# First stage of a decoder layer: all its loads on one queue in order of use, and keys, then values of three context tiles ahead of the norm of x

## The chip, the core and the metric

The kernel runs on one core of a Trainium2 chip. The core has five engines with a queue of instructions each: TensorE (PE in the profile, with its weight loads as PEld), VectorE (DVE), ScalarE (ACT), GpSimd (POOL) and SyncE (SP), which here only issues transfers. Each engine takes its own queue strictly in order; between engines there are semaphores. Transfers (DMAs) are issued from the queues of SP, ACT and POOL and are carried by 16 DMA engines that the core's queues share. Matmul results go to PSUM banks, which DVE or ACT must empty before PE can write them again.

The metric is the device time of one execution, in microseconds (us), as the median of several runs. Clock figures in the profile are shares of TensorE's full speed as granted to it.

## What is computed

One decoder layer on x of 16 x 64 x 512 numbers (n, c, l) and a context of 16 x 64 x 512, all float32. Cut to what matters:

```
xn = layernorm(x)                                   # over l
q  = transpose(xn, (2, 0, 1))                       # l, n, c
p  = softmax(einsum('lnc,lmc->lnm', q, q) / 8)      # 512 small attentions of 16 rows
x  = x + xn + transpose(einsum('lnm,lmc->lnc', p, q), (1, 2, 0))

h  = layernorm(x)
k  = rmsnorm(ctx @ Wk.T) * k_norm_w                 # 1024 rows, 8 heads of 128
v  = ctx @ Wv.T
qq = rmsnorm(h @ Wq.T) * q_norm_w                   # 32 heads of 128
x  = x + softmax(qq k / sqrt(128)) v @ Wo.T         # four query heads for each key head

x  = x + mixture_of_experts(layernorm(x))           # 16 experts, 4 for a row, and a shared one
```

The change concerns the first five lines and the lines of k and v: everything that runs before the queries of the second attention.

## The kernel before

All names are of one function, `decoder_layer`. The 1024 rows of context are cut into 8 tiles of 128 rows (NT = 8), each held with the contracted 512 on the partitions in four chunks (DC = 4). A scheduler places the instructions: program order sets dependencies and priorities, and the scheduler moves what is ready ahead in each engine's queue, so that for instance a matmul of a later tile can stand between the steps of an attention. The queues it fixes are then executed in order.

**Loads.** x goes to `xs`: partitions 0 to 63 take c with the first half of l, partitions 64 to 127 c with the second half. Eight transfers of 256 KB do it (line 133), issued from ACT's queue (S). On SP's queue (nc.sync) go context tile 0 (line 124), the key weights `wk_sb` in two halves of 1 MB (line 130), context tile 1, the value weights `wv_sb` in two halves (line 140), then the query weights of groups 0 and 1 (line 168). Each half of wk or wv holds 512 columns, that is four of the eight heads. POOL's queue loads small constants. Context tiles lie in a pool of two buffers (`two`, tag "ctx"), so tile i + 2 can be loaded when tile i has been used.

**`keys_values(i)`** works on context tile i: eight matmuls (two halves of four) against wk (line 213), whose two results ACT squares (line 218) and DVE sums and copies (lines 219, 220); eight matmuls against wv (line 224), whose results ACT copies (line 228); then the keys' root mean square (lines 230 to 232), eight transposes (line 236) and ACT's scaled copies into `kT` (line 237). A float32 matmul appears in the profile as two recorded passes, so 8 matmuls are `x16` there; a float32 transpose is one record. The results take turns in three PSUM banks (`mm_bank`).

**`split_norm`** is the layer norm of x. DVE takes statistics of each of 16 n (lines 176, 177); since a row's 512 numbers lie half on one partition and half on another, a small matmul joins the two halves' means (line 181), and a second one their deviations (line 189); ACT takes the root (line 191), DVE the reciprocal (line 193) and the 16 normalizations (line 199). The first call writes `xg`, the layout in which all 16 n of eight neighbouring l stand together, so that an attention can start only after the last of the 16. After each, POOL adds the normalized part to xs (line 298).

**`batch_attention(q)`** runs 64 of the 512 small attentions: transposes of xf (line 251), scores (line 259), scaling and maximum on DVE (lines 264, 269), exponentials on ACT (line 272), division on DVE (lines 276, 277), transposes of the probabilities (line 283), ACT's copy (line 285), products (line 287) and DVE's addition to xs (line 292). There are eight calls.

**The order of the stage**: keys_values(0), the norm of x, keys_values(1), then four times an attention, keys_values(i + 2) and another attention; POOL then sends xs away (lines 308, 309), `split_norm` runs again into xn, the query weights are loaded, keys_values(6) and (7) follow, and xn is transposed to `xnT` (line 319), from which the queries are computed (line 357). The expert stage at the end has lines from 760 on.

Of the kernel before, what the change touches and what calls it, by code (L numbers as in the profile page):

```python
# [23 lines left out]
F32 = mybir.dt.float32  # L24
# [5 lines left out]
P = 128  # L30
N, C, L = 16, 64, 512
NT = N * C // P
DC = L // P
# [15 lines left out]
def decoder_layer(  # L49
# [24 lines left out]
    nc = tc.nc  # L74
    V, S, T, G = nc.vector, nc.scalar, nc.tensor, nc.gpsimd
# [4 lines left out]
    wqp = ctx.enter_context(tc.tile_pool(name="wqp", bufs=2))  # L80
# [6 lines left out]
    def bank(tag, bufs):  # L87
        return psum.tile([P, 512], F32, tag=tag, name=tag, bufs=bufs)

    def mm_bank():  # L90
        return bank("mm", 3)

    def tr_bank():
        return bank("tr", 2)

    def sc_bank():
        return bank("sc", 3)
# [6 lines left out]
    v = [p.tile([P, NT, KVH // 2 * HD], F32, tag="v", name="v") for p in (kvp0, kvp)]  # L104
# [6 lines left out]
    two = p1.enter_context(tc.tile_pool(name="two", bufs=2))  # L111
# [5 lines left out]
    wk_sb = one.tile([P, DC, KVH * HD], F32, tag="wk", name="wk_sb")  # L117
    wv_sb = one.tile([P, DC, KVH * HD], F32, tag="wv", name="wv_sb")

    ctx_tiles = {}  # L120

    def load_ctx(i):
        ct = two.tile([P, DC, P], F32, tag="ctx", name="ct")
        nc.sync.dma_start(ct, ctxt[i])
        ctx_tiles[i] = ct

    load_ctx(0)
    for h in range(2):
        cols = slice(h * 512, (h + 1) * 512)
        nc.sync.dma_start(wk_sb[:, :, cols], wk[:, :, cols])  # L130
    for q in range(4):
        for h in range(2):
            S.dma_start(
                xs[h * C : (h + 1) * C, 4 * q : 4 * q + 4, :],
                x[4 * q : 4 * q + 4, :, h * LH : (h + 1) * LH].rearrange("n c l -> c n l"),
            )
    load_ctx(1)
    for h in range(2):
        cols = slice(h * 512, (h + 1) * 512)
        nc.sync.dma_start(wv_sb[:, :, cols], wv[:, :, cols])  # L140

    ident = const.tile([P, P], F32, tag="ident", name="ident")
    make_identity(nc, ident)
# [22 lines left out]
    def load_wq(g):  # L166
        w = wqp.tile([P, DC, GRP * HD], F32, tag="wq", name="wq_sb")
        nc.sync.dma_start(w, wq[g])
        wq_tiles[g] = w
# [31 lines left out]
            )  # L201


    def keys_values(i):
        ct = ctx_tiles.pop(i)
        if i + 2 < NT:
            load_ctx(i + 2)
        kraw = two.tile([P, KVH, HD], F32, tag="kraw", name="kraw")
        ss = small.tile([P, KVH], F32, tag="ss", name="ss")
        for h in range(2):  # L210
            kp = mm_bank()
            for d in range(DC):
                T.matmul(  # L213
                    kp, ct[:, d, :], wk_sb[:, d, h * 512 : (h + 1) * 512],
                    start=(d == 0), stop=(d == DC - 1),
                )
            kh = kraw[:, 4 * h : 4 * h + 4, :]
            S.activation(kh.rearrange("p h d -> p (h d)"), kp, AF.Square)
            V.tensor_reduce(ss[:, 4 * h : 4 * h + 4], kh, AX.X, ALU.add)
            V.tensor_copy(kh.rearrange("p h d -> p (h d)"), kp)  # L220
        for h in range(2):
            vp = mm_bank()
            for d in range(DC):
                T.matmul(  # L224
                    vp, ct[:, d, :], wv_sb[:, d, h * 512 : (h + 1) * 512],
                    start=(d == 0), stop=(d == DC - 1),
                )
            S.copy(v[h][:, i, :], vp)
        rk = small.tile([P, KVH], F32, tag="rk", name="rk")
        S.activation(rk, ss, AF.Sqrt, bias=eps_sb, scale=1.0 / HD)  # L230
        V.reciprocal(rk, rk)
        V.tensor_mul(kraw, kraw, rk.unsqueeze(2).to_broadcast([P, KVH, HD]))
        for h in range(2):
            tp = tr_bank()
            for j in range(4):
                T.transpose(tp[:, j * P : (j + 1) * P], kraw[:, 4 * h + j, :], ident)
            S.activation(
                kT[h][:, :, i * P : (i + 1) * P],
                tp.rearrange("p (j t) -> p j t", j=4), AF.Copy, scale=kw_sb,
            )  # L240


    def batch_attention(q):
        g0 = q * GE * LE

        def group(g, rows=slice(0, P)):
            return xf[rows, (q * GE + g) * P : (q * GE + g + 1) * P]

        qp = tr_bank()
        for g in range(GE):  # L250
            T.transpose(qp[:, g * P : (g + 1) * P], group(g), ident)
        qt = two.tile([P, GE, P], F32, tag="qt1", name="qt1")
        S.copy(qt.rearrange("p g c -> p (g c)"), qp)
        probs = []
        for h in range(2):
            hs = slice(h * C, (h + 1) * C)
            sp = sc_bank()
            for g in range(GE):
                T.matmul(
                    sp[:, g * P : (g + 1) * P], group(g, hs), group(g, hs),  # L260
                    start=True, stop=True,
                )
            pr = two.tile([P, GE, P], F32, tag="pr", name="pr", bufs=3)
            V.scalar_tensor_tensor(
                pr, sp.rearrange("p (g m) -> p g m", g=GE), C**-0.5,
                blocks_sb.unsqueeze(1).to_broadcast([P, GE, P]), ALU.mult, ALU.add,
            )
            nm = small.tile([P, GE], F32, tag="nm", name="nm")
            V.tensor_reduce(nm, pr, AX.X, ALU.max, negate=True)
            rs = small.tile([P, GE], F32, tag="rs", name="rs")  # L270
            for g in range(GE):
                S.activation(
                    pr[:, g, :], pr[:, g, :], AF.Exp, bias=nm[:, g : g + 1],
                    accum_out=rs[:, g : g + 1],
                )
            V.reciprocal(rs, rs)
            V.tensor_mul(pr, pr, rs.unsqueeze(2).to_broadcast([P, GE, P]))
            probs.append(pr)
        mp = sc_bank()
        for h in range(2):  # L280
            tp = tr_bank()
            for g in range(GE):
                T.transpose(tp[:, g * P : (g + 1) * P], probs[h][:, g, :], ident)
            pt = two.tile([P, GE, P], F32, tag="pt1", name="pt1")
            S.copy(pt.rearrange("p g n -> p (g n)"), tp)
            for g in range(GE):
                T.matmul(
                    mp[h * C : (h + 1) * C, g * P : (g + 1) * P],
                    qt[:, g, h * C : (h + 1) * C], pt[:, g, :], start=True, stop=True,
                )  # L290
        xv = xs[:, :, g0 : g0 + GE * LE].rearrange("p n (g e) -> p g n e", e=LE)
        V.tensor_add(xv, mp.rearrange("p (g n e) -> p g n e", g=GE, e=LE), xv)

    keys_values(0)
    split_norm(lambda n: xg[:, :, n, :], xs)
    for n in range(N):
        xv = xs[:, n, :].rearrange("p (g e) -> p g e", e=LE)
        G.tensor_add(xv, xv, xg[:, :, n, :])
    keys_values(1)
    for i in range(4):  # L300
        batch_attention(2 * i)
        keys_values(i + 2)
        batch_attention(2 * i + 1)
    for h2 in range(2):
        for h in range(2):
            rows, cols = slice(h2 * C, (h2 + 1) * C), slice(h * LH, (h + 1) * LH)
# [3 lines left out]
    split_norm(lambda n: xn[:, n, :], xs)  # L310
    load_wq(0)
    load_wq(1)
    keys_values(6)
    keys_values(7)
    for n0 in range(0, N, 4):
        for k in range(2):
            tp = tr_bank()
# [696 lines left out]
```

## Time and profile before

| what | value |
|---|---|
| median of 3 runs | 1096.88 us (1095.32 to 1097.59) |
| the profiled execution: its time | 1095.54 us |
| its span (first to last instruction) | 1093.8 us |
| mean granted clock of TensorE | 0.966 |
| PE busy, 0 to 20 us | 6.13 us |
| PE busy, 20 to 40 us | 15.34 us |
| PE busy, 40 to 60 us | 14.37 us |
| PE busy, 160 to 200 us | 39.34 of 40 us |
| first transposes of xn (line 319) | 194.16 us |
| first statistics of x on DVE (line 176) | 12.09 us |
| ACT's issues of x (line 133) | 0.75 to 15.5 us |

The span runs from the first to the last recorded instruction, and the time lies 1.74 us above it. Times within the profile are counted from the span's start. A row of a timeline gives the start, the duration, engine, line and operation, `out<-in` with the sizes, how many instructions were merged into it, and in brackets how long the engine had stood idle before it and what released it. A row of a windows table gives for a stretch of time its length, then busy time and number of instructions of PE, PEld, DVE, ACT and POOL, and then the granted clock, the busy share of the DMA engines and what they moved in GB/s. Matmuls are pipelined, so a busy engine need not run at its peak.

### The profile page before, as it was taken

The page shows a single profiled execution, that of the slowest core. Times are in us where ns is not written, and L with a number is a line of the kernel's source. Part 1 is how long each engine was busy: PE and PEld are TensorE (multiplying, and loading weights), DVE is VectorE, ACT ScalarE, POOL GpSimd, SP SyncE. Part 2 cuts the span into 40 slices and gives each one's busy share as a digit, 9 for nine tenths or more (in the row PEclk, how much of TensorE's full clock was granted, in tenths as well). Part 3 has the DMA queues.
Part 4 walks back from the last instruction along what each step waited for, and adds up shares of the span by engine and source line. Part 5 has one row for each costly group of instructions (what it writes and reads, how often), then busy time and mean ns, then how long its engine had stood idle before and what let it go on. Part 6 is the DMA issues. An engine that isn't in the chain of part 4 may idle for free. (4 is left out here: it accounts for less than half of the span.)

```text
span 1093.8 us, 13537 instructions
## 1 busy us (share of the span) xinstructions
PE 1007.2 (92%) x4556; PEld 704.4 (64%) x4556; DVE 533.7 (49%) x1112; ACT 414.7 (38%) x1130; POOL 344.5 (31%) x356
## 2 busy tenths in 40 slices
PE   3799999799999999999999989879799999999974
PEld 1355554587888888888888867767564455545431
DVE  1735557746664756556564566657567211111100
ACT  1156663255544544445454453332220122222220
POOL 2400001312332424225143342352352443444232
PEclk9999999899999999999999999988789999999997
DMA  9200003110110201102011110000022966655643
GB/s 249 99 20 10 10 10 78 78 40 1 39 40 1 78 1 39 39 34 102 1 39 39 40 39 1 30 30 20 29 33 88 396 155 148 148 122 104 155 106 54
DMA packets 28378, 74.96 MB, mean 69 GB/s; under 512 B 4560, under 2 KB 8704, under 8 KB 26256
## 3 DMA queue, kind: packets, MB, share of 16 engines
q1 hardware_dynamic: 15792, 49.81, 13.4%
q0 software_dynamic: 10336, 22.13, 9.9%
q10 hardware_dynamic: 2176, 2.10, 0.8%
q8 instruction: 38, 0.62, 0.2%
q14 instruction: 36, 0.29, 0.1%
HBM read 98.90 MB, written 16.02 MB: 105 GB/s over the span
## 5 line engine op out<-in xcount | busy, mean ns | idle before, releaser
L886 PE MATMUL sc<-w,xt 128*128 128x512 f32 x288 | 131.6, 601 | 1.4 <-ACT xt L880 1.4
L404 ACT ACTIVATE square<-qraw 128x128 f32<-128x128 f32 x256 | 79.2, 309 | 82.6 <-DVE qraw L398 43.3
L334 POOL TENSOR_TENSOR sat<-at 128x256 f32<-128x256 f32 x32 | 26.2, 818 | 254.6 <-ACT at L474 254.6
L911 POOL DMA_INDIRECT out_dram<-y,idx x36 | 56.8, 1577 | 121.3 <-DMA out_dram<-y,idx 59.3
L886 PEld LDWEIGHTS sc<-w,xt 128*128 128x128 f32 x288 | 52.8, 193 | 55.2 <-issue 53.3
L357 PE MATMUL mm<-wo_t,sat 128*128 128x256 f32 x256 | 70.6, 401 | 13.0 <-POOL sat L335 13.0
L891 DVE TENSOR_TENSOR z<-sc,z 128x256 f32<-128x256 f32 x36 | 15.2, 423 | 132.1 <-ACT z L890 132.1
L357 PE MATMUL mm<-wq_t,xns 128*128 128x256 f32 x256 | 72.7, 393 | 6.1 <-DVE xns L335 4.7
L357 PE MATMUL mm<-wo_sb,at 128*128 128x256 f32 x256 | 72.8, 406 | 4.3 <-ACT at L474 4.3
L213 PE MATMUL mm<-wk_sb,ct 128*128 128x512 f32 x128 | 62.4, 623 | 14.2 <-DMA wk_sb<-in_wk_dram 14.2
L436 PEld LDWEIGHTS sc<-kT,qt 128*128 128x128 f32 x512 | 62.1, 193 | 19.1 <-ACT qt L421 12.3
L357 PE MATMUL mm<-wq_sb,xnT 128*128 128x256 f32 x256 | 70.5, 381 | 2.6 <-DVE su L396 2.6
L441 DVE SCALAR_TENSOR_TENSOR prob<-sc,mask_sb 128x512 f32<-128x512 f32 x32 | 22.0, 687 | 103.8 <-PE sc L436 103.8
L436 PE MATMUL sc<-kT,qt 128*128 128x64 f32 x512 | 69.4, 282 | 1.6 <-ACT qt L421 1.4
L906 PE MATMUL mm<-w,zt 128*128 128x512 f32 x144 | 68.2, 596 | 2.6 <-DVE zt L899 2.1
L224 PE MATMUL mm<-wv_sb,ct 128*128 128x512 f32 x128 | 60.5, 612 | 9.9 <-DVE kraw L220 6.9
L357 PEld LDWEIGHTS mm<-wo_t,sat 128*128 128x128 f32 x256 | 50.6, 200 | 22.3 <-POOL sat L335 15.2
L357 PEld LDWEIGHTS mm<-wo_sb,at 128*128 128x128 f32 x256 | 51.2, 205 | 13.2 <-ACT at L474 6.3
L357 PEld LDWEIGHTS mm<-wq_t,xns 128*128 128x128 f32 x256 | 47.5, 194 | 12.2 <-POOL wq_sb L344 4.9
L890 ACT ACTIVATE z<-sc 128x256 f32<-128x256 f32 x36 | 13.8, 383 | 108.4 <-PE sc L886 108.4
L906 PEld LDWEIGHTS mm<-w,zt 128*128 128x128 f32 x144 | 26.9, 190 | 35.8 <-issue 32.1
L870 POOL DMA_INDIRECT xg<-rows_d,idx x38 | 37.2, 980 | 39.9 <-DVE weight L840 18.2
(252 smaller groups left out, 2030.8 us busy)
## 6 DMA issues: line engine op xcount, KB each, us to landing
w<-in_wg_dram SPq DMA_DIRECT2D x38, 512.0 KB
w<-in_wu_dram SPq DMA_DIRECT2D x38, 512.0 KB
w<-in_wd_dram SPq DMA_DIRECT2D x38, 512.0 KB
wq_sb<-in_wq_dram SPq DMA_DIRECT2D x8, 1024.0 KB
wo_sb<-in_wo_dram SPq DMA_DIRECT2D x8, 1024.0 KB
ct<-in_ctxt_dram SPq DMA_DIRECT2D x8, 256.0 KB
xs<-in_x_dram ACTq DMA_DIRECT2D x8, 256.0 KB
wk_sb<-in_wk_dram SPq DMA_DIRECT2D x2, 1024.0 KB
```

The costliest lines, as they stand in the source:

```text
L213: T.matmul(kp, ct[:, d, :], wk_sb[:, d, h * 512 : (h + 1) * 512], start=(d == 0), stop=(d == DC - 1),)
L224: T.matmul(vp, ct[:, d, :], wv_sb[:, d, h * 512 : (h + 1) * 512], start=(d == 0), stop=(d == DC - 1),)
L334: engine.tensor_add(s[:, 0], a21, a22)
L357: T.matmul(dst, left[:, k, :], right[:, k, :], start=k == 0, stop=k == 1)
L404: S.activation(square, raw[:, h, :], AF.Square, accum_out=q_ss[g][:, 2 * u + j, h : h + 1])
L436: T.matmul(sp[:, at : at + C], qt[:, b, 2 * hp : 2 * hp + 2, :], kT[g // 4][:, g % 4, k0 : k0 + C], start=True, stop=True,)
L441: V.scalar_tensor_tensor(pr, sp.rearrange("p (a k) -> p a k", a=8), HD**-0.5, mask_sb.unsqueeze(1).to_broadcast([P, 8, C]), ALU.mult, ALU.add,
L870: G.indirect_dma_start(xg, None, rows_d, bass.IndirectOffsetOnAxis(idx[:, b : b + 1], axis=0))
L886: T.matmul(hp, xt[:, d, :], w1_tiles[buffer(j)][:, :, d, :], start=(d == 0), stop=(d == DC - 1))
L891: V.tensor_mul(z, hp[:, FI:], z)
L906: T.matmul(op, zt[:, c, :], w2_tiles[buffer(j)][:, c, :], start=(c == 0), stop=(c == FI // P - 1))
L911: G.indirect_dma_start(out, bass.IndirectOffsetOnAxis(idx[:, b : b + 1], axis=0), y, None, bounds_check=NT * P - 1, oob_is_err=False, comp ...
```

## The change

All loads of the first stage are issued on SP's queue, in the order in which they are used: context 0, the first half of wk in four pieces of 256 KB (one for each chunk of the contracted dimension), its second half, context 1, half of x, context 2, the rest of x, wv, contexts 3 to 5. Four context tiles get a place of their own, `ctx_early`, which is one of the two buffers of the pool of query weights (8 KB on each partition); the second load of query weights into that buffer must wait until they have been used.

`keys_values` is parted into `keys(i)` and `values(i)`. Keys of tiles 0, 1, 2, then values of 0, 1, 2 now stand ahead of the norm of x. Tiles 3, 4 and 5 follow after the second, fourth and sixth attention in program order, tiles 6 and 7 after the second norm, keys first.

```diff
+    ctx_early = wqp.tile([P, 4, DC, P], F32, tag="wq", name="ctx_early")
+
     def load_ctx(i):
-        ct = two.tile([P, DC, P], F32, tag="ctx", name="ct")
+        ct = ctx_early[:, i] if i < 4 else two.tile([P, DC, P], F32, tag="ctx", name="ct")
         nc.sync.dma_start(ct, ctxt[i])
         ctx_tiles[i] = ct
 
+    halves_of = [slice(h * 512, (h + 1) * 512) for h in range(2)]
     load_ctx(0)
-    for h in range(2):
-        cols = slice(h * 512, (h + 1) * 512)
-        nc.sync.dma_start(wk_sb[:, :, cols], wk[:, :, cols])
+    for d in range(DC):
+        nc.sync.dma_start(wk_sb[:, d, halves_of[0]], wk[:, d, halves_of[0]])
+    nc.sync.dma_start(wk_sb[:, :, halves_of[1]], wk[:, :, halves_of[1]])
+    load_ctx(1)
     for q in range(4):
         for h in range(2):
-            S.dma_start(
+            nc.sync.dma_start(
                 xs[h * C : (h + 1) * C, 4 * q : 4 * q + 4, :],
                 x[4 * q : 4 * q + 4, :, h * LH : (h + 1) * LH].rearrange("n c l -> c n l"),
             )
-    load_ctx(1)
-    for h in range(2):
-        cols = slice(h * 512, (h + 1) * 512)
+        if q == 1:
+            load_ctx(2)
+    for cols in halves_of:
         nc.sync.dma_start(wv_sb[:, :, cols], wv[:, :, cols])
+    for i in range(3, 6):
+        load_ctx(i)
...
-    def keys_values(i):
-        ct = ctx_tiles.pop(i)
-        if i + 2 < NT:
-            load_ctx(i + 2)
+    def keys(i):
+        ct = ctx_tiles[i]
         kraw = two.tile([P, KVH, HD], F32, tag="kraw", name="kraw")
...
+    def values(i):
+        ct = ctx_tiles.pop(i)
+        if 4 <= i < NT - 2:
+            load_ctx(i + 2)
+        for h in range(2):
+            vp = mm_bank()
+            for d in range(DC):
+                T.matmul(
+                    vp, ct[:, d, :], wv_sb[:, d, h * 512 : (h + 1) * 512],
+                    start=(d == 0), stop=(d == DC - 1),
+                )
+            S.copy(v[h][:, i, :], vp)
...
-    keys_values(0)
+    for part in (keys, values):
+        for i in range(3):
+            part(i)
     split_norm(lambda n: xg[:, :, n, :], xs)
     for n in range(N):
         xv = xs[:, n, :].rearrange("p (g e) -> p g e", e=LE)
         G.tensor_add(xv, xv, xg[:, :, n, :])
-    keys_values(1)
-    for i in range(4):
-        batch_attention(2 * i)
-        keys_values(i + 2)
-        batch_attention(2 * i + 1)
+    for i in range(8):
+        batch_attention(i)
+        if i in (1, 3, 5):
+            keys(3 + i // 2)
+            values(3 + i // 2)
...
     load_wq(0)
     load_wq(1)
-    keys_values(6)
-    keys_values(7)
+    for part in (keys, values):
+        for i in (6, 7):
+            part(i)
```

## The prediction

> **What bounds the kernel now.** The page's first part comes first: TensorE (PE) is busy for most of the span, so time is won or lost where it waits. Next the clock and the 40 slices, whose first two and a later pair are thin. What the change touches lies ahead of 200 us, so the timeline of PE for that stretch follows. [...]
>
> ```profile
> PE 1007.2 (92%) x4556; PEld 704.4 (64%) x4556; DVE 533.7 (49%) x1112; ACT 414.7 (38%) x1130; POOL 344.5 (31%) x356
> ```
> ```profile
> 13.81 6.13 PE L213 MATMUL mm<-wk_sb,ct 128*128 128x512 f32 x8 [13.81 <-DMA wk_sb<-in_wk_dram]
> 20.36 3.70 PE L213 MATMUL mm<-wk_sb,ct 128*128 128x512 f32 x8 [0.41 <-DMA wk_sb<-in_wk_dram]
> 27.15 3.70 PE L224 MATMUL mm<-wv_sb,ct 128*128 128x512 f32 x8 [3.09 <-DMA wv_sb<-in_wv_dram]
> 32.06 3.70 PE L224 MATMUL mm<-wv_sb,ct 128*128 128x512 f32 x8 [1.22 <-DVE kraw L220]
> ...
> 37.34 0.29 PE L181 MATMUL tr<-mh,halves_sb 128*128 128x16 f32 x2
> ...
> 53.02 5.32 PE L224 MATMUL mm<-wv_sb,ct 128*128 128x512 f32 x8 [5.63 <-DVE kraw L220]
> 58.18 1.04 PE L236 MATMUL tr<-ident,kraw 128*128 128x128 f32 x8
> 59.15 0.71 PE L259 MATMUL sc<-xf 64*128 64x128 f32 x4
> ```
>
> PE waits 13.8 + 0.4 + 3.1 + 1.2 + 5.6 = 24.1 us before the first attention at 59.15. Each program matmul against wk or wv is two recorded passes; eight passes take 3.70 us, but 6.13 in the first group and 5.32 after the 5.63 us idle: cold starts, costing 2.4 and 1.6 us. From 59.15 to 193.8 PE has no idle of note. The windows by 20 us show it (PE busy first, its granted clock and DMA share near the end):
>
> ```profile
> 60.00:80.00 20.00, 20.00 (x84) 10.89 (x82) 8.99 (x15) 10.83 (x29) 0.00 (x0) 1.00 0.03 9
> 80.00:100.00 20.00, 19.97 (x103) 11.93 (x102) 12.07 (x21) 13.19 (x43) 0.00 (x0) 1.00 0.04 12
> ```
>
> The 5.6 us idle has its cause on VectorE (DVE), in whose queue the copies of keys 1 stand behind the 16 normalizations of x, which POOL's adds accompany; the second norm, without POOL beside it, takes half:
>
> ```profile
> 40.20 10.98 DVE L199 TENSOR_SCALAR xf<-xs,mean,rstd 128x256 f32<-128x256 f32 x16
> ```
> ```profile
> 183.49 5.24 DVE L199 TENSOR_SCALAR xf<-xs,mean,rstd 128x256 f32<-128x256 f32 x16
> ```
>
> Last, the loads by windows of 1 us (last column GB/s):
>
> ```profile
> 3.00:4.00 1.00, 0.00 (x0) 0.00 (x0) 0.00 (x0) 0.00 (x0) 1.00 (x3) 1.00 0.96 236
> 9.00:10.00 1.00, 0.00 (x0) 0.00 (x0) 0.00 (x0) 0.00 (x0) 0.47 (x1) 1.00 1.06 300
> 17.00:18.00 1.00, 1.00 (x2) 0.33 (x1) 0.00 (x0) 0.00 (x0) 0.00 (x0) 1.00 1.10 191
> ```
>
> The engines are full from 2 us on, at about 280 GB/s (190 from 16 to 20 us): bandwidth, shared by wk with x, sets when wk arrives.
>
> **The change, part by part.** Units: a wk or wv matmul is 0.86 us warm (two passes of 0.43, the spacing of their weight loads), 1.7 cold; a context tile is 8 for keys, 8 for values, and 8 transposes (58.18 to 59.15: 0.96). I follow the built kernel's order on PE.
>
> *Loads.* All go on SP in the order context 0, wk half 0 in four pieces, wk half 1, context 1, half of x, context 2, rest of x, wv, contexts 3 to 5, wq. ScalarE loses its eight issues (0.75 to 15.5 us); these covered nothing, since its first work comes at 19.98. SP gains eleven issues of 0.3 to 0.7 us each (four wk pieces in place of one, eight of x); past the eighth each waits for the one eight before it, so 2 MB, 7 us of transfer, stay queued: no gap. First bytes come at 2.0 as now. Context 0 with one piece is 0.52 MB: 1.9 us at 280 GB/s, plus 0.6 for completion (my choice), so PE starts at **4.5**, not 13.8. The whole wk, with context 0 and POOL's small loads, is 2.66 MB: 9.5 us, there at 12.1. The second wq load waits for values 3 to free the buffer that the early contexts borrow, with contexts 6 and 7 queued behind it; they are needed some 40 us later, so nothing.
>
> A rule speaks against splitting: the Trainium skill, "DMA: Bandwidth & Descriptors", section "Anatomy of one DMA", fits one DMA (on POOL's path) as about 2.0 us plus bytes over 436 GB/s. Five pieces in series would be 5 x 2.6 = 13 us and wk half 0 no earlier than now; the gain would shrink by some 5 us. The rows show 236 to 300 GB/s while several are queued, so the fixed part overlaps, and I take the rows.
>
> *Keys, then values, of three tiles.* Keys 0 half 0 begins at 4.5: six cold passes of 0.85, two warm, to 10.5. It waits 1.6 for wk half 1 (12.1), and ends at 15.5. Then 16 matmuls of keys (13.8), 24 of values (20.6), 3 sets of transposes (2.9): 52.8. Loads at 280 GB/s: context 2 at 17.7 (needed at 23), wv halves at 25.2 and 29.0 (needed at 31 and 35). At 190 GB/s for x alone wv is 3.5 later, just covered. Bounds for small waits of the transposes on DVE's key work: 0 to 3; I take 0.7. **53.5.**
>
> The cold start itself: "TensorE: Matmul & The Clock Gate", section "Part 1: The HAM clock gate", puts the warm-up at about 3.4 us, which would cost 1.7; the first group's passes stay at 0.85 until 18.9, 5.1 us, so I use 2.5. The rule would add 0.8 us of gain.
>
> *The norm goes later.* Its statistics stand on DVE among the key work (16 x 0.39 us), but its mean matmul is queued on PE behind all 24 values, so it starts at 53.5 instead of 37.3. From mean matmul to first normalization took 37.34 to 40.20, 2.9 us; POOL's adds still run beside, so 11.0 more: attention 0 starts at **67.4**. PE has keys 3 and one matmul of values 3 in between (9 x 0.86 = 7.7 plus 0.6), then idles 5.6 us: the old stall returns in a new place, with its cold restart (1.7). Behind that wait stand values 3 and all later work.
>
> *Account.* At 67.4 + 1.7 = 69.1 PE has done 57 matmuls and 3 transpose sets. Before, at 59.15, 32 and 2. The missing 25 x 0.86 + 0.96 = 22.5 put the old kernel at the same point at 81.6. **Saved: 12.5 us.**
>
> *Attention stage.* Before, 72 matmuls and 4 sets lie between 59.15 and the last score-value product (end 170.7); now 53 and 3. The fill is thinner, but half of the attentions before already had only four matmuls between scores and the first transpose of probabilities (93.39 to 97.10, transposes at 97.13: no wait), as most have now. DVE and ACT need a period of about 9.1 us (92.95 to 98.6 for two halves, plus 3.4 from the transposes at 89.53 to 92.95); PE's own work is (111.5 - 19 x 0.86 - 0.96) / 8 = 11.8. Cost: 0 by this; bounds 0 to 15.6.
>
> *Second norm.* It was covered by 24 matmuls, 23.5 us (170.7 to the first transposes of xn at 194.16). Now 18 and two sets are left behind the last product: 18.1 us. Its chain, from that product: eleven matmuls, 9.5, to the mean matmul (DVE's add, 16 x 0.39 of statistics and 1.4 of keys 7 are done by 9.0), 2.9 to the first normalization, 5.24 for sixteen: 17.7. So 0, with thin cover: a late chain would cost up to 2. Behind it the order on every engine is as before but for how the transposes of xn mix with the first query matmuls, and PE carries the rest (99.6 of 100 us busy from 300 to 400), so nothing later eats the saving.
>
> *Sum.* The profiled run took 1095.54 (span 1093.8): 1095.54 - 12.5 = 1083.0. It lies 1.3 under the median, 1096.88; on the median's footing I predict **1084.4**.
>
> **Rivals.** *Transfers stay the bound* (0.22). If the single queue holds 190 GB/s throughout, wk is there at 16.6 (4.5 late) and wv's second half at 41.4 (about 2 late): saving 5.8, time 1091. For: that row, in which PE and x's 1 KB rows are active together. Against: the other rows at 280 to 300.
>
> *The attention stage keeps its length* (0.12; slower). Were its 111.5 us set by the DVE and ACT chain, less fill would only make PE wait: 67.4 + 111.5 + 18.1 = 197.0 against 194.16 for the transposes of xn, 3 us slower, 1100. Price: 1.95 us of PE wait in each of eight attentions; from 1.6 the saving is gone. Against: the 9.1 us period, and DVE and ACT busy under 14 of 20 us.
>
> *The gain is returned* (0.04) at the two norms, the starts or between: within 2 us, 1096. That the loads don't come in order is excluded: one queue issues them.
>
> **Numbers.** My forecast has 0.62, from 1080 to 1088. Its best end has PE starting 0.6 earlier, no wait for wk, no small waits, no cold restart: 4.6 more, 1079.8. The range 1079 to 1094 takes in the transfer case and leaves out the slower one and the tails. What this kernel can tell from no change is about 0.2%, 2.2 us. Faster 0.84 (forecast and transfers), same 0.04, slower 0.12.
>
> **What would show it.** PE's first wk matmul at 4 to 5.5 us; the last of values 2 at 52 to 55; the mean matmul straight after; 16 normalizations still about 11 us; an idle of 5 to 6 us ended by DVE's normalization; attention 0 at 66 to 69; full PE windows up to the transposes of xn at about 181 (194.16 before). I am wrong if PE idles on wk or wv beyond 2 us, or shows gaps inside the eight attentions.

## The result, and the profile after

| | before | after |
|---|---|---|
| median (15 runs each) | 1096.11 us (1085.9 to 1099.71) | 1088.81 us (1082.02 to 1092.03) |
| ratio, 95% interval | 1 | 0.9939 [0.9912, 0.9965] |
| profiled execution: time, span | 1095.54, 1093.8 | 1090.55, 1088.8 |
| first attention's transposes on PE | 59.15 | 72.53 |
| first transposes of xn on PE | 194.16 | 188.01 |
| from there to the end of the span | 899.6 | 900.8 |

The change wins 0.6%, some 6.7 us (the ratio is that of the means; the medians lie 7.3 us apart). The prediction expected 12.5. The changed kernel's page begins:

```profile
PE 1011.1 (93%) x4556; PEld 708.5 (65%) x4556; DVE 533.0 (49%) x1112; ACT 409.5 (38%) x1126; POOL 344.0 (32%) x356
```

The instruction counts of PE and DVE are unchanged, yet PE is busy 3.9 us longer: some passes became slower, which points to the clock. PE's timeline of the first stage (start, duration, instruction, count, idle before it with its releaser):

```profile
4.76 5.46 PE L219 MATMUL mm<-wk_sb,ctx_early 128*128 128x512 f32 x6 [4.76 <-DMA wk_sb<-in_wk_dram]
10.47 1.18 PE L219 MATMUL mm<-wk_sb,ctx_early 128*128 128x512 f32 x2 [0.26 <-DMA wk_sb<-in_wk_dram]
15.48 10.64 PE L219 MATMUL mm<-wk_sb,ctx_early 128*128 128x512 f32 x18 [3.83 <-DMA wk_sb<-in_wk_dram]
...
58.64 0.29 PE L189 MATMUL tr<-mh,halves_sb 128*128 128x16 f32 x2
...
72.53 1.11 PE L262 MATMUL tr<-ident,xf 128*128 128x128 f32 x4 [5.56 <-DVE xf L207]
73.58 3.09 PE L270 MATMUL sc<-xf 64*128 64x128 f32 x16
76.60 7.39 PE L247 MATMUL mm<-wv_sb,ctx_early 128*128 128x512 f32 x14
...
188.01 1.04 PE L333 MATMUL tr<-ident,xf 128*128 128x128 f32 x8
```

PE starts at 4.76 instead of 13.81. The key half that begins at 15.48 was forecast for 12.1: it waits 3.83 us for wk's second half, not 1.6. Values of tile 2 end at 58.6 (forecast 53.5), with the mean matmul directly behind them. DVE had its input ready at 36.4, so it stood 22 us in PE's queue behind values. The old wait for DVE's normalizations is back in front of the first attention, 5.56 us long. The 14 passes at 76.60 take 7.39 us, where 14 warm ones would take about 6.2 (16 take 7.03 from 26.84 on). The mean matmul's input on DVE:

```profile
36.21 0.17 DVE L187 COPY mh<-mv 128x16 f32<-128x16 f32 x1
```

Windows of 1 us show the clock (length, busy time of PE, PEld, DVE, ACT, POOL, then granted clock, DMA share, GB/s). First the kernel after, then the kernel before:

```profile
14.00:15.00 1.00, 0.00 (x0) 0.00 (x0) 0.00 (x0) 0.00 (x0) 0.00 (x0) 0.51 1.13 160
20.00:21.00 1.00, 1.00 (x3) 0.48 (x2) 0.00 (x0) 0.00 (x0) 0.00 (x0) 0.58 1.13 196
...
72.00:73.00 1.00, 0.47 (x2) 0.47 (x3) 1.00 (x3) 0.00 (x0) 1.00 (x2) 0.52 0.00 0
78.00:79.00 1.00, 1.00 (x2) 0.34 (x1) 0.97 (x3) 0.98 (x5) 0.00 (x0) 0.56 0.00 0
```
```profile
49.00:50.00 1.00, 0.00 (x0) 0.00 (x0) 1.00 (x2) 0.00 (x0) 1.00 (x2) 0.75 0.00 0
56.00:57.00 1.00, 1.00 (x3) 0.37 (x3) 0.00 (x0) 0.00 (x0) 0.00 (x0) 0.84 0.00 0
```

Between the two windows of each pair the clock is 0.50. A mean of 0.75 says that the drop to one half came in the middle of its window, at 49.5; 0.84 says that the rise came a third into its own, at 56.3. So before, the half clock lasted 6.8 us, of which 3.5 fell into the idle time (work came at 53.02): it cost half of the other 3.3, the 1.6 us that the prediction read off. In the kernel after, it lasts from 14.0 to 20.8 and from 72.0 to 78.9: 6.8 us again, twice, but now 5.4 and 6.3 us of it fall on work and cost 2.7 and 3.2 us. (The very first passes also take 0.85 us each, up to about 10.5, though the clock column reads 1.00 there: the trace has no clock record before 10.61.)

That closes the account. At the transposes of xn the forecast was 181.7 and the trace has 188.01, 6.3 late. Up to the last value matmul it is 5.1 late: 3.4 by the start of the second key half, 2.7 by the clock, less 1.0, of which 0.7 had been set aside for small waits that did not come. The restart at the first attention adds 3.2 - 1.7 = 1.5. Together 6.6, which is 0.3 more than measured.

Two questions remain for experiments: why wk's second half is late, and whether the loads or the new order bring the gain.

### The profile page after: what moved, and what is told of

Same layout as the page of the kernel before. It is cut to its first block, busy times and chain, and to the rows that moved or that the text cites. A ratio compares the mean times of both kernels' runs of the same rounds, so it can differ in the third digit from the quotient of the medians.

```text
span 1088.8 us, 13528 instructions
## 1 busy us (share of the span) xinstructions
PE 1011.1 (93%) x4556; PEld 708.5 (65%) x4556; DVE 533.0 (49%) x1112; ACT 409.5 (38%) x1126; POOL 344.0 (32%) x356
## 4 chain that ended last, share of the span: by engine, by line
PE 81%; DVE 6%; POOL 4%; DMA 3%; issue 3%; ACT 2%; SPq 0%; DVEq 0%; POOLq 0%; ACTq 0%
PE mm L371 28%; PE sc L900 11%; PE sc L450 6%; PE mm L920 5%; PE mm L247 5%; PE mm L219 5%; PE sc L371 5%; PE sc L482 3%; PE tr L433 2%; DMA out_dram<-y,idx 2%; PE sc L270 2%; PE sc L298 2%; PE sc L774 1%; PE tr L892 1%; POOL table_d L731 1%
## 5 line engine op out<-in xcount | busy, mean ns | idle before, releaser
L371 PE MATMUL mm<-wo_t,sat 128*128 128x256 f32 x256 | 71.8, 406 | 13.6 <-POOL sat L349 13.6
L371 PE MATMUL mm<-wo_sb,at 128*128 128x256 f32 x256 | 71.8, 402 | 4.3 <-ACT at L488 3.1
L371 PEld LDWEIGHTS mm<-wq_sb,xnT 128*128 128x128 f32 x256 | 45.1, 192 | 8.2 <-DVE su L410 3.8
L435 ACT ACTIVATE qt<-tr,qw_sb 128x512 f32<-128x512 f32 x64 | 43.1, 691 | 14.1 <-PE tr L433 14.1
```

Source lines behind the costliest of these rows:

```text
L371: T.matmul(dst, left[:, k, :], right[:, k, :], start=k == 0, stop=k == 1)
L435: S.activation(qt.rearrange("p b h q -> p h b q"), tp.rearrange("p (h b q) -> p h b q", h=GRP, b=2), AF.Copy, scale=qw_sb,)
```

## Experiments

Theory A: x, and what else follows on the same queue, delays wk's second half. Theory B: the constants that POOL loads at the same time (0.34 MB, of which the prediction had made only their bytes, about 1.1 us) delay it. Each variant starts from the kernel after. "Second half" is PE's start on wk's second half, in brackets the idle before it; "attention" and "xn" are the two landmarks of the table above. Landmarks are from one profiled execution of each kernel. Each ratio is to runs of the kernel before that were taken beside it (medians 1094.76 to 1096.11), so it is not the quotient of two medians of the table.

| kernel | second half | attention | xn | median (runs) | ratio to before, 95% |
|---|---|---|---|---|---|
| before | 20.36 (0.41) | 59.15 | 194.16 | 1096.11 (15) | 1 |
| after | 15.48 (3.83) | 72.53 | 188.01 | 1088.81 (15) | 0.9939 [0.9912, 0.9965] |
| e1: x behind wv | 14.50 (2.92) | 71.44 | 186.87 | 1085.58 (20) | 0.9917 [0.9894, 0.9940] |
| e2: constants behind | 11.68 (0.41) | 66.09 | 181.27 | 1078.70 (4) | 0.9846 [0.9816, 0.9875] |
| f2: one constant behind | 13.49 (1.16) | 67.90 | 184.67 | 1085.53 (1) | |
| f3: the small ones behind | 14.79 (2.87) | 70.76 | 187.37 | 1087.06 (1) | |
| g3: constants amid wk | 14.29 (3.66) | 71.37 | 186.87 | 1087.08 (1) | |
| e3: x on ACT's queue | 19.48 (4.19) | 78.13 | 194.19 | 1095.48 (20) | 0.9993 [0.9971, 1.0016] |
| e4: norm between | 17.06 (5.65) | 59.78 | 178.60 | 1077.01 (4) | 0.9810 [0.9761, 0.9860] |
| f1: e4 and constants behind | 10.69 (0.51) | 51.64 | 170.49 | 1064.79 (4) | 0.9722 [0.9665, 0.9780] |
| e5: loads only | 13.29 (0.11) | 53.44 | 186.64 | 1084.98 (19) | 0.9931 [0.9906, 0.9956] |
| e6: order only | 19.18 (0.26) | 80.37 | 197.11 | 1093.99 (20) | 1.0010 [0.9985, 1.0035] |

### x behind wv (e1)

```diff
     load_ctx(1)
+    load_ctx(2)
+    for cols in halves_of:
+        nc.sync.dma_start(wv_sb[:, :, cols], wv[:, :, cols])
     for q in range(4):
         for h in range(2):
             nc.sync.dma_start(xs[...], x[...])
-        if q == 1:
-            load_ctx(2)
-    for cols in halves_of:
-        nc.sync.dma_start(wv_sb[:, :, cols], wv[:, :, cols])
```

> All eight loads of x stand behind wv instead of between contexts 1 and 2; nothing else is moved. Theory A (the rows of x behind wk half 1 in the queue hold up its last packets): PE's wait for wk half 1 falls from 3.8 us to 1.5 or less (it is there by 12.5 us, not 15.5), the clock does not drop, the last of values 2 ends at 53 to 55 instead of 58.6, attention 0 starts at about 67.5 instead of 72.5, the time is some 5 us below the changed kernel's. Theory B (POOL's small loads hold it up): wk half 1 still at 15 to 16 us, attention 0 at 72 to 73.

The second half starts at 14.50, 1.0 us earlier, and the clock still drops (12.8 to 19.7). Kernels whose loads are the same up to that point differ by more: 15.48 (after), 17.06 (e4), and 13.29 in e5. So what follows on the queue explains at most a small part: A falls as the main cause.

### Constants behind (e2)

All of POOL's eight constants go to SP's queue, behind contexts 3 to 5.

```diff
-    G.dma_start(halves_sb, halves)
+    nc.sync.dma_start(halves_sb, halves)
...
-    G.dma_start(before_sb, before.partition_broadcast(P))
+    nc.sync.dma_start(before_sb, before.partition_broadcast(P))
```

> The eight constant loads leave POOL's queue and stand on SP behind contexts 3 to 5; nothing else is moved. Theory B: wk half 1 is there by 13 us, PE waits 2 us or less, no clock drop, attention 0 at about 68. Theory A: wk half 1 at 14.5 to 15.5 (the 0.3 MB no longer moved early is worth 1 us at most), attention 0 at 71 to 73, time within 2 us of the changed kernel's.

PE's timeline of e2:

```profile
4.86 6.41 PE L219 MATMUL mm<-wk_sb,ctx_early 128*128 128x512 f32 x8 [4.86 <-DMA wk_sb<-in_wk_dram]
11.68 7.99 PE L219 MATMUL mm<-wk_sb,ctx_early 128*128 128x512 f32 x18 [0.41 <-DMA wk_sb<-in_wk_dram]
...
66.09 1.11 PE L262 MATMUL tr<-ident,xf 128*128 128x128 f32 x4 [5.57 <-DVE xf L207]
...
181.27 1.04 PE L333 MATMUL tr<-ident,xf 128*128 128x128 f32 x8
```

The wait of 3.83 us is 0.41, the clock does not drop (18 passes take 7.99 us, not 10.64), and xn is reached at 181.27, where the forecast stood (181.7). That match is partly luck: the mean matmul starts 1.3 us before its forecast (52.19, said 53.5), and the restart, with the clock at half from 65.0 to 71.8, costs 2.9 us instead of 1.7. B holds in this run, and f1 repeats it (10.69). Against the spread of 13.3 to 17.1 with the constants beside, the delay is between 1.6 and 6.4 us, 3.8 against the run of after. The size is what surprises: for 0.34 MB the bytes had said 1.1. It is not the sum of bytes: in the kernel after, the windows from 2 to 12 us add up to 2.82 MB, more than the 2.70 MB of context 0, wk and the constants together, and still PE is not released by wk's second half before 15.48.

The landings in the traces say more. Each of these loads has 16, and PE can go on only after the last. For wk's second half the fifteenth and the last came at 13.03 and 15.44 in the kernel after and at 14.17 and 17.02 in e4, but at 11.48 and 11.63 in e2 and at 9.92 and 10.64 in f1. Of the 3.8 us between after and e2, then, 2.3 are one sixteenth of the load that comes late and 1.5 the rest of it. With all constants on POOL's queue the last landing does not always trail: by 0.7 us in e1 (13.74, 14.45), by 0.1 in e5 (13.16, 13.25). That is most of the scatter between these kernels. Why one share is held up in some executions, the traces do not show.

### Which of the constants (f2, f3, g3)

f2 moves only the 128 KB table that is broadcast to all partitions:

```diff
-    G.dma_start(before_sb, before.partition_broadcast(P))
+    nc.sync.dma_start(before_sb, before.partition_broadcast(P))
```

> Of POOL's constants only the broadcast one of 128 KB (before_sb) goes behind contexts 3 to 5; the other seven stay. If bytes hold up wk half 1 (128 of 313 KB): its start on PE moves from 15.5 to about 14. If the broadcast is special: to 12.5. If it is the many small packets: no move, 15 to 16.

f3 moves the mask, qw, kw, gate and bias alone:

```diff
-        G.dma_start(mask_sb[h * C : (h + 1) * C, :], mask)
+        nc.sync.dma_start(mask_sb[h * C : (h + 1) * C, :], mask)
...
-    G.dma_start(bias_sb, bias.partition_broadcast(P))
+    nc.sync.dma_start(bias_sb, bias.partition_broadcast(P))
```

> Of POOL's constants only the five small ones (mask, two scales, gate, bias: 57 KB in packets of 4 to 256 bytes) go behind contexts 3 to 5; the three large ones (256 KB) stay. If the small packets hold up wk half 1: it starts on PE at 12.5 or sooner. If bytes do: 15. If the broadcast does: 15 to 16.

Each is one execution, and 13.49 and 14.79 lie within the scatter of the kernels that leave all constants on POOL's queue (13.3 to 17.1), so they neither name a culprit nor clear one. g3 puts all eight on SP, between the pieces of wk's first half and its second half, to tell POOL's queue from the small packets:

```diff
         nc.sync.dma_start(wk_sb[:, d, halves_of[0]], wk[:, d, halves_of[0]])
+    nc.sync.dma_start(halves_sb, halves)
...
+    nc.sync.dma_start(bias_sb, bias.partition_broadcast(P))
     nc.sync.dma_start(wk_sb[:, :, halves_of[1]], wk[:, :, halves_of[1]])
```

> The eight constants stand on SP's own queue, right ahead of wk half 1, so that all their bytes must pass before it. If it is POOL's queue beside SP's that holds wk half 1 up (packets of two queues taken in turn): half 1 starts on PE at 12.4 to 13.2 (11.7 with the constants behind, plus 0.31 MB at 350 GB/s, 0.9 us). If these loads are slow in themselves, for their small packets or the broadcast, whatever queue issues them: 15 us or later.

It does not tell them apart. SP's queue in g3, and then g3's windows:

```profile
8.39 0.61 SPq L152 DMA_DIRECT2D wk_sb<-in_wk_dram  x1
```
```profile
8.00:9.00 1.00, 1.00 (x3) 0.47 (x2) 0.00 (x0) 0.00 (x0) 0.00 (x0) 1.00 0.20 34
9.00:10.00 1.00, 1.00 (x3) 0.40 (x2) 0.00 (x0) 0.00 (x0) 0.00 (x0) 1.00 0.34 23
```

The second half of wk was issued at 8.39 instead of 3.09: nine issues of about 0.5 us now stand before it on SP, and those past the eighth load also wait for an earlier one to land. The DMA engines stood nearly empty meanwhile. The 14.29 thus comes from a late issue, which is another cause than the one in question.

### x back on ACT's queue (e3)

```diff
-            nc.sync.dma_start(
+            S.dma_start(
                 xs[h * C : (h + 1) * C, 4 * q : 4 * q + 4, :],
```

> The loads of x go back to ACT's queue; all else is as in the changed kernel. If what the one queue brings is that wk need not share the bandwidth with x (my prediction's reckoning), wk half 1 comes at 18 to 20 us, attention 0 starts at 75 to 77, and the time is 3 to 5 us above the changed kernel's. If the order on PE alone brings the gain, the time stays within 1.5 us of it.

The gain is gone: 0.9993, xn at 194.19. PE's timeline of e3, and SP's queue with a row of the waits (total, times, longest):

```profile
7.28 2.04 PE L219 MATMUL mm<-wk_sb,ctx_early 128*128 128x512 f32 x2 [7.28 <-DMA wk_sb<-in_wk_dram]
...
19.48 9.45 PE L219 MATMUL mm<-wk_sb,ctx_early 128*128 128x512 f32 x16 [4.19 <-DMA wk_sb<-in_wk_dram]
```
```profile
6.84 0.66 SPq L135 DMA_DIRECT2D wk_sb<-in_wk_dram  x1
```
```profile
SPq L135 <- DMA xs<-in_x_dram: 3.2, 1, 3.2
```

Two things happen at once. x shares the DMA engines from the start (first pass at 7.28, not 4.76), and the issue of wk's second half on SP waits 3.2 us for a load of x on ACT: this program gives the loads of both queues eight semaphores in turn, so wk's second half, the tenth, waits until the second load, the first of x, has landed. The run shows that one queue in order of use is worth the whole gain with this order of work; how much of it is sharing and how much is the late issue, it does not show.

### The norm between keys and values (e4), and both mends (f1)

```diff
-    for part in (keys, values):
-        for i in range(3):
-            part(i)
+    for i in range(3):
+        keys(i)
     split_norm(lambda n: xg[:, :, n, :], xs)
...
+    for i in range(3):
+        values(i)
     for i in range(8):
         batch_attention(i)
```

> The norm of x stands between keys 0 to 2 and values 0 to 2 in program order. My theory (the stall of 5.6 us before attention 0 and its cold restart come from the mean matmul queued behind all 24 values): mean matmul at about 43.5 instead of 58.6, normalizations done by 57.5 under the values, attention 0 at about 59.5 with no idle above 1 us and full clock; by equal work that is 8 to 9 us saved on the changed kernel, first transposes of xn at about 179.5 instead of 188.0. Rival (that stage is set by the later fill, which is only moved): attention 0 early, but the time within 2 us of the changed kernel's, with PE idle later, inside the attentions or at the second norm.

PE's timeline of e4:

```profile
43.88 0.29 PE L189 MATMUL tr<-mh,halves_sb 128*128 128x16 f32 x2
...
45.96 13.98 PE L247 MATMUL mm<-wv_sb,ctx_early 128*128 128x512 f32 x32
59.78 0.60 PE L262 MATMUL tr<-ident,xf 128*128 128x128 f32 x4
```

The mean matmul no longer stands behind 24 matmuls of values; they now cover the normalizations, and the first attention starts without an idle and at full clock, although in this execution the second half of wk came later than in any other kernel with these loads (17.06). xn is reached 9.4 us earlier than after. f1 adds e2's move of the constants, with the two that the keys and the mean matmul need, kw and halves, placed behind context 2:

```diff
         if q == 1:
             load_ctx(2)
+            nc.sync.dma_start(kw_sb, kw)
+            nc.sync.dma_start(halves_sb, halves)
```

> Norm between keys and values as in the run before it, and in addition the constants off POOL's queue: the keys' scale and the matrix of the means behind context 2 on SP, the other six behind contexts 3 to 5. Theory (two separate losses that add up: POOL's loads delay wk half 1 and chill PE; the mean matmul behind the values stalls attention 0): PE's wait for wk half 1 under 1 us, attention 0 at about 54 (59.8 with the norm moved alone), first transposes of xn at about 172.5, a ratio to the kernel before of 0.974 to 0.980. Rival (one stall hides the other, only the longer counts): transposes at 177 to 179, ratio as with the norm alone, 0.981.

PE's timeline of f1:

```profile
10.69 7.99 PE L219 MATMUL mm<-wk_sb,ctx_early 128*128 128x512 f32 x18 [0.51 <-DMA wk_sb<-in_wk_dram]
...
35.75 0.29 PE L189 MATMUL tr<-mh,halves_sb 128*128 128x16 f32 x2
...
51.64 0.60 PE L262 MATMUL tr<-ident,xf 128*128 128x128 f32 x4
...
170.49 1.04 PE L334 MATMUL tr<-ident,xf 128*128 128x128 f32 x8
```

Both losses are gone and they add: 6.7 us (e2) and 9.4 (e4) of 188.01 would give 171.9, measured 170.49. f1 takes 1064.79 us, 2.8% less than before (0.9722, a little better than the 0.974 to 0.980 expected), and beats both kernels.

### Loads only (e5) and order only (e6)

e5 keeps the new loads and puts the old order back:

```diff
-    for part in (keys, values):
-        for i in range(3):
-            part(i)
+    keys(0)
+    values(0)
     split_norm(lambda n: xg[:, :, n, :], xs)
...
+    keys(1)
+    values(1)
+    for i in range(4):
+        batch_attention(2 * i)
+        keys(i + 2)
+        values(i + 2)
+        batch_attention(2 * i + 1)
```

> The changed kernel's loads with the old order of computation (keys and values of 0, norm, keys and values of 1, then in turn with the attentions). If the loads bring the gain: PE starts at 4.5, waits some 7 us for the means of x, attention 0 starts at about 51 instead of 59.2, transposes of xn at 186 to 189, time as the changed kernel's within 2 us. If the order brings it: transposes at 192 to 195, time within 2 us of the kernel before.

PE's timeline of e5:

```profile
21.23 1.94 PE L234 MATMUL tr<-ident,kraw 128*128 128x128 f32 x8 [4.11 <-DVE kraw L230]
27.73 0.58 PE L189 MATMUL tr<-mh,halves_sb 128*128 128x16 f32 x2 [4.56 <-issue]
...
53.44 0.60 PE L262 MATMUL tr<-ident,xf 128*128 128x128 f32 x4
```

PE waits for the keys of tile 0 and for x's statistics (4.1, 4.6 and 1.0 us up to 29.3; DVE has the means ready at 27.6) and runs at half clock from 20.4 to 34.1. The first attention nevertheless starts without an idle. The ratio, 0.9931, is that of the whole change, 0.9939, well within either interval.

e6 keeps the new order and puts the old loads back:

```diff
-    for d in range(DC):
-        nc.sync.dma_start(wk_sb[:, d, halves_of[0]], wk[:, d, halves_of[0]])
-    nc.sync.dma_start(wk_sb[:, :, halves_of[1]], wk[:, :, halves_of[1]])
-    load_ctx(1)
+    for cols in halves_of:
+        nc.sync.dma_start(wk_sb[:, :, cols], wk[:, :, cols])
...
-            nc.sync.dma_start(
+            S.dma_start(
                 xs[h * C : (h + 1) * C, 4 * q : 4 * q + 4, :],
```

> The new order of computation with the old loads (wk in two halves on SP, x on ACT, context 1, wv, contexts 2 to 5); the constants on POOL's queue. PE starts at 13.8 as before. If the order brings the gain by itself: attention 0 at about 75 (16 matmuls more done by then than the old kernel at 59.2, less the cold restart), transposes of xn at 190 to 192, time 2 to 4 us below the kernel before. If the loads bring it all: transposes at 193 to 196, time within 2 us of the kernel before.

PE's timeline of e6:

```profile
31.14 3.68 PE L216 MATMUL mm<-wk_sb,ctx_early 128*128 128x512 f32 x4 [4.83 <-DVE kraw L223]
...
80.37 1.11 PE L259 MATMUL tr<-ident,xf 128*128 128x128 f32 x4 [5.57 <-DVE xf L204]
```

With the old loads the copies of keys stand behind x's statistics on DVE and empty no PSUM banks, so PE waits 4.83 us, and the stall ahead of the first attention is there as well. Ratio 1.0010, no difference. The gain is the loads'. The order as made moves the norm's stall to another place and brings nothing by itself.

## Why the prediction was half right

**Right.** PE's start (4.76, said 4.5): the pieces of wk overlap, as the rows of several queued transfers had said and the one-transfer price had not. The mean matmul directly behind the values, the normalizations beside POOL's adds, the idle behind them: DVE's rows of the kernel after have the forecast 11.0:

```profile
61.50 10.97 DVE L207 TENSOR_SCALAR xf<-xs,mean,rstd 128x256 f32<-128x256 f32 x16
```

and from 72.53 to 188.01 no gap was added. The attentions cost nothing for having less work between them: landmark to landmark the forecast was 181.7 - 67.4 = 114.3, the trace has 115.5, and the difference is within the 1.5 us of the restart. wv did not make PE wait, and the second norm cost nothing. The rival of an attention stage that keeps its length is thereby out, and so is the return of the gain at other places.

**Wrong: the step "The whole wk, with context 0 and POOL's small loads, is 2.66 MB: 9.5 us, there at 12.1".** Bytes over a mean rate gave no price to loads that another queue has under way at the same time. PE had it at 15.48, and e2 and f1 show that without these loads 11.7 and 10.7 are reached. Through which resource they hold up wk stays open; the landings show only that one share of the load came 2.4 us behind the others (13.03, 15.44). The prediction's own sign of being wrong, an idle of PE on wk beyond 2 us, was there: 3.83.

**Wrong in size: the term "its cold restart (1.7)".** It was taken from the row of before, where half of the cold time lay in the idle. The right term is half of the cold time that falls on work: 3.2 us there, and 2.7 more at 15.48, where the prediction had no restart since it had a wait of only 1.6. In e2, where the wait is 0.4, this second loss is gone with it.

The rival "transfers stay the bound" gave a saving of 5.8 and measured is 6.15, but only its first half came: wk was late (15.48, it said 16.6), wv was not. Its reason, a low rate throughout, is not what the windows of the kernel after show:

```profile
9.00:10.00 1.00, 1.00 (x2) 0.00 (x0) 0.00 (x0) 0.00 (x0) 0.00 (x0) 1.00 0.95 355
10.00:11.00 1.00, 0.74 (x2) 0.35 (x2) 0.00 (x0) 0.00 (x0) 0.00 (x0) 1.00 0.97 365
11.00:12.00 1.00, 0.65 (x2) 0.00 (x0) 0.00 (x0) 0.31 (x1) 0.00 (x0) 1.00 1.08 348
```

So it came near the time for another reason. The measured 1088.81 lies just above the forecast's own 1080 to 1088, inside the range that had been widened to 1094 for this rival.

**Not foreseen by any case:** the order of the forecast could have been doubted for itself. The prediction priced the move of the mean matmul and the return of the stall, but compared only with before. e4 shows that the same work with the norm between keys and values is worth 9.4 us more.

## What to carry to other kernels

When a first matmul waits for its weights, take every other load out of that stretch, small constants on other queues included: here they cost 3.8 us between two executions (1.6 to 6.4 over all pairs) in place of the 1.1 that their bytes say. Place a chain of short dependent steps, such as a norm's, ahead of the long independent work that can cover it, not behind; where an in-order queue decides, the small matmul that starts the chain is the one to move. And when one change alters loads and order together, run each alone: here one brought all the gain.

## What the runs showed of the hardware

**The clock moves on a fixed grid.** Read off the windows as above, the phases of half clock up to the first attention last 3.4 us (e6's first, f3's first), 6.8 (before, after twice, e1 twice, e2, e4, g3 twice, e3's first), 10.2 (f2, and the second of e3, e6 and f3) or 13.7 (e5): multiples of 3.41. In the kernel after, the two drops lie 58.0 us apart, 17 times 3.41. The Trainium skill, "TensorE: Matmul & The Clock Gate", section "Part 1: The HAM clock gate", has a free-running window of 3413 ns, and these lengths agree. They do not agree with its statement that the drop needs an idle window of some 3.4 us: the half clock came 1.3 us (e1), 2.1 (before) or 2.4 (after, first) behind PE's last work, 5.1 in after's second case, while before's idle of 3.09 us had none.

Laid over PE's busy time, the grid shows what the drop goes by. Up to 600 us the twelve traces have 41 drops, and each ended a window in which PE was busy less than half the time (at most 49%: e1, 9.42 to 12.84). Of 1946 windows of full clock without a drop at their end, one was under half (44%, before, at 213.3). The 3.09 us of before fell on two windows, each of them 55% busy, and so cost nothing. For the rise no such line came out: all 53 rises followed a window at least 88% busy, but nine such windows stayed cold. So a restart has no fixed price: it depends on where the work falls against the grid.

**Rows of x are slow.** In the kernel after, the windows from 12 to 24 us, with x under way, moved 153 to 230 GB/s at a DMA share above 1.0 (160 and 196 in the two shown above); in e1, with contexts and wv under way from 13 to 16, 381 to 387:

```profile
14.00:15.00 1.00, 0.50 (x1) 0.50 (x2) 0.00 (x0) 0.00 (x0) 0.00 (x0) 0.50 1.05 387
```

x's loads write 1 KB rows on 64 partitions, those of contexts and wv 2 KB rows on 128; which of the two matters was not tried.

**Whole times scatter by the expert stage.** From the first transposes of xn to the end, before, after, e2, e3, e4, f2, f3 and g3 took 897.2 to 901.9 us (before 899.6, after 900.8); e1, e5, e6 and f1 took 890.7 to 894.4, with the same work left. A row of PE's waits parts the two groups: a gather ahead of the experts' transposes (shown of before, then of after), which the second group does not have. Its 2.6 to 5.7 us are a part of the 7.2 us between the groups' means:

```profile
PE tr L878 <- DMA xg<-rows_d,idx: 4.0, 1, 4.0
```
```profile
PE tr L892 <- DMA xg<-rows_d,idx: 4.9, 1, 4.9
```

Since one profile can have it and the next not, a difference of two profiled times says little here; the landmarks of the changed stage do. Why the gather is late in some executions was not tried.
